# Perceiver layer on one core: the second product with the values moved behind the second burst of scores

## The chip, the cores and the metric

The kernel runs on one core of a Trainium2 chip. The metric is the time of one execution in microseconds (us) on the device, as a median over several runs. Lower is better. All arithmetic is in float32.

## The reference, cut to what matters

There are 32 sequences of 64 rows with 256 features. Each has a context of 1601 rows. Three blocks follow one another, each added to x: attention over the context with 16 heads of 16 features, an attention whose weights depend on positions, and a feed-forward block with a shared part and experts. The change touches the first one:

```python
qh = _split_heads(q @ wq_w.T + wq_b)          # q is the normalised x
kh = _split_heads(k @ wk_w.T + wk_b)          # k and v are the context
vh = _split_heads(v @ wv_w.T + wv_b)
scores = jnp.einsum('bhqd,bhkd->bhqk', qh, kh) / jnp.sqrt(jnp.float32(D_K))
scores = jnp.where(mask, scores, jnp.float32(-1000000000.0))
attn = jax.nn.softmax(scores, axis=-1)
out = jnp.einsum('bhqk,bhkd->bhqd', attn, vh)
```

## The kernel before

The context's 1601 rows (keys) are cut into 13 blocks of 124 and stand on the partitions once they have become scores. The work goes by halves: half n is a sequence b and a group c of eight heads, so there are 64 halves. The loop at line 766 runs over n = 0 to 62. One pass of it, called a stretch here, prepares scores for half n+1, turns the scores of half n into exponentials, and multiplies the exponentials of half n-1 with the values. The order on TensorE (PE), VectorE (DVE), ScalarE (ACT) and GpSimd (POOL) is the order in which the code records the instructions (`manual_schedule`, line 730); each engine works its queue strictly from the front.

TensorE's work in a stretch, in order, with the names that the profile shows:

- `values(n-1, 0)` (line 625), the first product of the exponentials with the values: 52 matmuls into the tile `pvs`, in column tiles (four matmuls side by side in four groups of 32 columns of the array).
- `project_keys(b+1, c, 0)`, tile `pk`: keys from the context. `product` (line 488) issues a projection either whole or in column tiles of 32 when `tiled` is true.
- `scores(n+1, 0)` (line 529): a burst of 16 matmuls in row tiles, tiles `psc`. Four key blocks for four pairs of heads, one bank of PSUM for each pair.
- `turned_maxima` (`pm`), a projection, `maxima_along_rows` (`pb`): the running maxima of half n are transposed, reduced by DVE (`mc`, line 601) and spread again.
- the steps of other layers that are due (`run`, line 695): generators that the agenda resumes at given stretches. They bring work such as `po`, `tr_q`, `tr_h`, `tr_f`.
- `values(n-1, 1)`, the second product, in column tiles.
- `scores(n+1, 1)`: the second burst, 20 matmuls. It has five key blocks; those of the fifth go to two banks of their own, called `more`. One is an ordinary bank. The other is `spare_pvs`, the second half of the tile `both` (lines 436 to 439) whose first half is `pvs`; the profile calls both halves `pvs`.
- projections of keys and values, whole, then the third burst `scores(n+1, 2)`, then projections in column tiles.

DVE takes the scores out of PSUM, adds the mask (line 570 for four blocks, line 563 for the fifth blocks) and updates the running maxima in `mrun` (line 587), in an order written out as strings. For the second burst it is one of these:

```python
    "A 0 m3 1 B 2 m8 3 m4 m5",
SOONER = "A 0 1 B 2 m8 3 m4 m5"
LATER = "A 0 m1 1 m2 B 2 m3 3 m8 m4 m5"
```

A digit is a bank with four blocks, m with a number is a maximum, A and B are the two banks with the fifth blocks. B is the one in `spare_pvs`. POOL subtracts the maxima (line 618), four pairs per half, and ACT takes the exponentials (line 623). ACT also copies projections out of PSUM with the bias (`kT`, line 507; `v`, line 524), copies `mb` (line 613) and starts the maxima (`mrun`, line 579). SyncE (SP) issues the loads of the context in four pieces per sequence, two sequences ahead (`piece_ahead`). Six banks of PSUM (`ps_x`) rotate among projections, scores and steps, so a matmul into a bank waits for whoever read it last.

Of the kernel before, what the change touches and what calls it, by code (L numbers as in the profile page):

```python
# [90 lines left out]
def perceiver_kernel(ctx: ExitStack, tc: tile.TileContext, a: dict[str, bass.AP], out: bass.AP):  # L91
# [16 lines left out]
    def mm_bank(name: str):  # L108
        return ps_mm.tile([P, 512], F32, tag="mm", name=name)
# [33 lines left out]
    def load_piece(b: int, g: int):  # L143
        c0, n = GROUPS[g]
        k0, kn = c0 * CHUNK, min(n * CHUNK, KEYS - c0 * CHUNK)
        ct = big.tile([P, 2, 4 * CHUNK], F32, tag="ct", bufs=5, name=f"ct_{b}_{g}")
        nc.sync.dma_start(
            out=ct[:, :, :kn],
            in_=a["ctxT"][b].rearrange("(c p) k -> p c k", p=P)[:, :, k0 : k0 + kn],
        )  # L150
        cts[b].append(ct)
# [269 lines left out]
    def pair_of(n: int, j: int):  # L421
        return prob[:CHUNK, place(n, j // 2), j % 2]
# [60 lines left out]
    def piece_ahead(b: int, g: int):  # L483
        if b < B:
            load_piece(b, g)
# [43 lines left out]
    def scores(n: int, g: int, then=None, order=None):  # L529

        b, c = halves[n]
        c0, nb = SCORED[g]


        more = [mm_bank(f"psc_{b}_{c}_{g}"), spare_pvs] if nb == 5 else None
        pss = [mm_bank(f"psc_{b}_{c}_{g}_{j}") for j in range(4)]
        for r in range(nb):
            for j in range(4):
                e, s = divmod(j, 2)[::-1]
                fifth = nb == 5 and r == 4 * s  # L540
                i = 4 if fifth else r - (nb == 5 and s == 0)
                ps, at = (more[e], s) if fifth else (pss[j], i)
                if fifth and j == 2:
                    tc.add_manual_dep(nc.tensor.nop().ins, mm.ins.name, IN_TURN, reason="banks")
                k0 = (c0 + i) * CHUNK
                product = nc.tensor.matmul(  # L546
                    ps[:CHUNK, at * P : (at + 1) * P],
                    lhsT=kTs[c][32 * j : 32 * j + 32, k0 : k0 + CHUNK],
                    rhs=qbd[b // 2][32 * j : 32 * j + 32, c, b % 2, :, :],
                    start=True, stop=True, tile_position=(32 * j, 0),  # L550
                )
                if fifth and j == 1:
                    mm = product
        held = then() if then else None
        for item in (order or ORDER[g]).split():
            if item == "t":
                if held is not None:
                    maxima_of_rows(*held)
            elif item[0] == "m":
                maximum(n, int(item[1:]))  # L560
            elif item in "AB":
                k, e = c0 + 4, "AB".index(item)
                nc.vector.tensor_tensor(  # L563
                    block_of(n, k)[:, :, e, :],
                    more[e][:CHUNK, : 2 * P].rearrange("p (r q) -> p r q", r=2),
                    madd_fifth[:CHUNK, None, :].to_broadcast([CHUNK, 2, P]), ALU.add,
                )
            else:
                j = int(item)
                nc.vector.tensor_tensor(  # L570
                    pair_of(n, j)[:, c0 : c0 + 4, :].rearrange("p k (e q) -> p k e q", e=2),
                    pss[j][:CHUNK].rearrange("p (k e q) -> p k e q", k=4, e=2),
                    madd[:CHUNK, c0 : c0 + 4, None, :].to_broadcast([CHUNK, 4, 2, S]), ALU.add,
                )
# [47 lines left out]
    def exponentials(n: int, j: int):  # L622
        nc.scalar.activation(pair_of(n, j), pair_of(n, j), AF.Exp)  # L623

    def values(n: int, r: int):

        b, c = halves[n]
        v = vs[b % 2]
        for k in range(NKC):
            kn = min(CHUNK, KEYS - k * CHUNK)  # L630
            for j in range(4):
                h = 4 * r + j
                nc.tensor.matmul(  # L633
                    pvs[32 * j : 32 * j + DK + 1, c, :, r, :],
                    lhsT=v[:kn, k, 8 * c + h, :],
                    rhs=pair_of(n, h // 2)[:kn, k, (h % 2) * S : (h % 2) * S + S],
                    start=(k == 0), stop=(k == NKC - 1), tile_position=(0, 32 * j),
                )
# [29 lines left out]
    def linear_factor(u: int):  # L668
        quarter, hc = divmod(u, NHC)
        nc.scalar.activation(  # L670
            gated_at(quarter, hc), half_unit(u, sw3), AF.Identity, bias=b3twice[:, hc : hc + 1]
        )
        linear.add(u)
# [29 lines left out]
    def finish_steps(b: int, stretch: int):  # L703

        t = b // 2
        if b % 2 == 0:
            oT[t] = work.tile([P, 2, 2, S], F32, tag="oT", name=f"oT_{t}")
        flat = "p c u r q -> p (c u r q)"
        nc.vector.transpose(turned_pvs.rearrange(flat), pvs.rearrange(flat))
        by_head = turned_pvs.rearrange("p c u r i -> p (c u r) i")  # L710
        rec = work.tile([P, 8], F32, tag="rec", name=f"rec_{b}")
        nc.vector.reciprocal(rec, by_head[:, :, DK])
        o = work.tile([P, 8, DK], F32, tag="o", name=f"o_{b}")
        nc.vector.tensor_tensor(
            o, by_head[:, :, :DK], rec[:, :, None].to_broadcast([P, 8, DK]), ALU.mult
        )
        nc.vector.transpose(oT[t][:, :, b % 2, :], o.rearrange("p (c n) i -> p c (n i)", c=2))
        if b % 2:
            at = steps_of(t)
            agenda[stretch - 1 + at[0]].append((t, span_steps(t, oT.pop(t))))  # L720
            held_at.add(stretch - 1 + at[SMALL])
        yield
# [39 lines left out]
        load_piece(1, g)  # L762
    last = len(halves) - 1

    extra = {3 * last - 3: (0,), 3 * last - 2: (1, 2, 4), 3 * last - 1: (5, 6)}
    for n, (b, c) in enumerate(halves[:-1]):
        if c == 0:
            piece_ahead(b + 2, 0)
            if b % 2 == 0 and b // 2 + 1 < NTILE:
                load_x(b // 2 + 1)  # L770
        if c and b % 2 == 0 and b // 2 + 1 < NTILE:
            agenda[3 * n].append((b // 2 + 1, query_steps(b // 2 + 1)))

        def project(f, *args):
            if b + 1 < B:
                f(b + 1, *args)

        def steps(g: int):
            run(3 * n + g)
            for u in extra.get(3 * n + g, ()):  # L780
                linear_factor(u)

        def taken_off():
            turned.extend(turned_maxima(n))
            return turned

        turned: list = []
        if n:
            values(n - 1, 0)
        project(project_keys, c, 0, True)  # L790
        if n:
            steps(-1)
            exponentials(n - 1, 3)
        if c:
            piece_ahead(b + 2, 1)
        scores(n + 1, 0, taken_off)
        if c:
            project(project_values, 3)
        else:
            project(project_keys, c, 1)  # L800
        m = maxima_along_rows(turned[1])
        less_maxima(n, 0, m, nc.gpsimd)
        held = 3 * n in held_at
        if not held:
            first_maxima(n + 1)
        run(3 * n)
        if n:
            values(n - 1, 1)
            if c == 0:
                agenda[3 * n + 1].append((b // 2, finish_steps(b - 1, 3 * n + 1)))  # L810
        for u in extra.get(3 * n, ()):
            linear_factor(u)
        if held:
            first_maxima(n + 1)
        else:
            for k in (1, 2) if c else (1, 2, 3):
                maximum(n + 1, k)

        scores(n + 1, 1, order=LATER if held else None if c else SOONER)
        exponentials(n, 0)  # L820
        if c:
            project(project_keys, c, 1)
            piece_ahead(b + 2, 2)
            project(project_values, 4)
            project(project_keys, c, 2)
            piece_ahead(b + 2, 3)
        else:
            project(project_keys, c, 2)
            for u in (0, 1):
                project(project_values, u)  # L830
        less_maxima(n, 1, m, nc.gpsimd)
        steps(1)
        exponentials(n, 1)

        less_maxima(n, 2, m, nc.gpsimd)
        scores(n + 1, 2)
        project(project_keys, c, 3, True)
        for u in (5, 6) if c else (2,):
            project(project_values, u, True)
        less_maxima(n, 3, m, nc.gpsimd)  # L840
        exponentials(n, 2)
# [177 lines left out]
```

## Time and profile before

| | |
|---|---|
| median of 3 runs | 1513.79 us (1511.66 to 1515.7) |
| the profiled execution | 1510.1 us, of which the span from first to last instruction is 1508.3 us |
| mean granted TensorE clock | 0.994 of full speed |
| instructions in the profile | 62981 |
| matmuls of L633 (both products with the values) | 212.3 us busy, 13312 records |
| matmuls of L546 into psc (scores) | 239.2 us busy, 6400 records |
| DVE L563 out of the half of `pvs` | 64 instructions, 415 ns each |

A float32 matmul leaves two records, so counts of records are twice those of matmuls. Busy time of TensorE counts overlapping matmuls once. "L546" is line 546 of the listing. The timeline merges equal instructions that follow each other: its columns are start, time from the first start to the last end, engine, line, operation, output and inputs, shape, and count; brackets tell idle time of the engine and what ended it.

### The profile page before, as it was taken

The numbers are of one execution on the slowest core, as the hardware profiler recorded it, in microseconds if no ns is written. First come the engines' busy times: TensorE is split into PE (matmuls) and PEld (weight loads), VectorE is DVE, ScalarE is ACT, GpSimd is POOL, SyncE is SP. The second block draws the span as 40 slices with busy tenths as digits, with TensorE's granted clock in tenths as the row PEclk, the third lists the DMA queues.
The fourth block names the chain that finished last, engine by engine and source line by source line (L and its number), as shares of the span: only waits on it lengthen the run. The fifth ranks groups of instructions, "written<-read, shape, count | busy, mean of one in ns | idle before, by whom it ended". The sixth has DMA issues, their size and how long they took to land.

```text
span 1508.3 us, 62981 instructions
## 1 busy us (share of the span) xinstructions
PE 1466.4 (97%) x28600; PEld 1059.0 (70%) x28600; DVE 1226.2 (81%) x2332; ACT 953.7 (63%) x1727; POOL 1120.2 (74%) x508
## 2 busy tenths in 40 slices
PE   8999999999999999999999999999999999988899
PEld 5676777777676767777777767777777777654587
DVE  4889898998989898989989899989899898973100
ACT  3565667676776767586767767676767666766411
POOL 1677787988878887879888888878798888852710
PEclk9999999999999999999999999999999999999999
DMA  5211111111111111111111111111111111005100
GB/s 179 56 37 46 36 47 46 38 48 50 50 50 47 43 43 43 37 53 37 49 51 50 50 47 52 34 44 37 52 46 40 50 50 33 2 9 161 60 29 28
DMA packets 52220, 73.95 MB, mean 49 GB/s; under 512 B 3828, under 2 KB 51184, under 8 KB 51824
## 3 DMA queue, kind: packets, MB, share of 16 engines
q1 hardware_dynamic: 51136, 69.13, 16.1%
q8 instruction: 225, 3.69, 1.0%
q10 hardware_dynamic: 816, 0.79, 0.2%
q14 instruction: 43, 0.35, 0.1%
HBM read 65.71 MB, written 4.19 MB: 46 GB/s over the span
## 4 chain that ended last, share of the span: by engine, by line
PE 58%; DVE 20%; POOL 11%; ACT 8%; issue 2%; DMA 0%; ACTq 0%; DVEq 0%; POOLq 0%
PE pv L492 14%; PE pk L492 13%; POOL prob L618 9%; DVE prob L570 8%; PE pvs L633 7%; PE psc L546 7%; DVE mrun L587 7%; PE py L949 4%; PE u L662 2%; PE pb L609 2%; PE ph L931 2%; DVE mc L601 2%; ACT prob L623 2%; ACT qbd L474 1%; PE psa L357 1%
## 5 line engine op out<-in xcount | busy, mean ns | idle before, releaser
L618 POOL TENSOR_TENSOR prob<-prob,mb 124x1664 f32<-124x1664 f32 x252 | 938.9, 3751 | 217.2 <-ACT mb L613 160.4
L570 DVE TENSOR_TENSOR prob<-psc,madd 124x512 f32<-124x512 f32 x768 | 505.4, 682 | 76.1 <-PE psc L546 75.8
L623 ACT ACTIVATE prob<-prob 124x1664 f32<-124x1664 f32 x256 | 407.1, 1590 | 214.9 <-POOL prob L618 212.0
L587 DVE TENSOR_TENSOR mrun<-prob,mrun 124x512 f32<-124x512 f32 x704 | 486.6, 691 | 31.1 <-ACT mrun L579 17.3
L492 PE MATMUL pk<-ct,wkT_sb 128*32 128x496 f32 (+1 forms) x2512 | 398.9, 519 | 7.5 <-DMA wkT_sb<-in_wkT 5.4
L492 PE MATMUL pv<-wvT_sb,ct 128*124 128x256 f32 x3524 | 386.1, 379 | 0.6 <-DVE prob L563 0.5
L492 PEld LDWEIGHTS pv<-wvT_sb,ct 128*124 128x124 f32 x3524 | 270.3, 132 | 108.1 <-issue 19.4
L546 PEld LDWEIGHTS psc<-qbd,kT 32*124 32x124 f32 x6400 | 201.0, 181 | 63.5 <-issue 19.2
L546 PE MATMUL psc<-qbd,kT 32*124 32x128 f32 x6400 | 239.2, 279 | 2.7 <-issue 1.4
L492 PEld LDWEIGHTS pk<-ct,wkT_sb 128*32 128x32 f32 (+1 forms) x2512 | 146.6, 126 | 118.3 <-issue 59.0
L633 PEld LDWEIGHTS pvs<-prob,v 124*17 124x17 f32 x13312 | 197.3, 98 | 29.9 <-issue 16.2
L633 PE MATMUL pvs<-prob,v 124*17 124x64 f32 x13312 | 212.3, 220 | 1.6 <-ACT prob L623 1.6
L507 ACT ACTIVATE kT<-pk,cols 128x372 f32<-128x372 f32 (+2 forms) x256 | 150.0, 586 | 81.9 <-PE pk L492 81.7
L524 ACT COPY v<-pv 124x512 f32<-124x512 f32 (+1 forms) x224 | 124.1, 554 | 85.4 <-PE pv L492 84.0
L323 ACT ACTIVATE sc<-sc,least 128x64 f32<-128x64 f32 x256 | 85.6, 342 | 2.1 <-DVE least L319 2.1
L951 DVE SCALAR_TENSOR_TENSOR ot<-py,prob 128x256 f32<-128x256 f32 x16 | 6.8, 425 | 75.7 <-PE py L949 66.1
L662 PE MATMUL u<-xfT,sw_sb 128*128 128x512 f32 x128 | 60.9, 624 | 3.6 <-ACT prob L689 2.7
L579 ACT COPY mrun<-prob 124x512 f32<-124x512 f32 x64 | 38.0, 593 | 38.3 <-DVE soft L306 35.3
L546 PE MATMUL pvs<-qbd,kT 32*124 32x128 f32 x256 | 55.2, 294 | 0.2 <-issue 0.2
L323 ACT ACTIVATION_READ_ACCUMULATOR sc<-sc,least 128x1 f32 x256 | 50.0, 195 | 0.0
L609 PEld LDWEIGHTS pb<-cst,mc 128*124 128x124 f32 x256 | 28.8, 135 | 29.3 <-DVE mc L601 23.8
L938 ACT ACTIVATE hT<-ph,cols 128x256 f32<-128x256 f32 x32 | 13.4, 471 | 56.3 <-PE ph L931 56.3
(126 smaller groups left out, 1249.3 us busy)
## 6 DMA issues: line engine op xcount, KB each, us to landing
ct<-in_ctxT SPq DMA_DIRECT2D x64, 372.0 KB, 3.2
ct<-in_ctxT SPq DMA_DIRECT2D x32, 496.0 KB, 3.7
ct<-in_ctxT SPq DMA_DIRECT2D x32, 361.0 KB, 3.2
w<-in_w SPq DMA_DIRECT2D x16, 256.0 KB, 7.2
x<-in_x SPq DMA_DIRECT2D x17, 128.0 KB, 2.7
x_kept<-x SPq DMA_DIRECT2D x16, 128.0 KB, 1.7
prob<-x_kept SPq DMA_DIRECT2D x8, 256.0 KB, 6.2
out<-ot SPq DMA_DIRECT2D x16, 128.0 KB, 1.9
```

Of the source, the lines that this page charges most:

```text
L323: nc.scalar.activation(sc[:, h, :], sc[:, h, :], AF.Exp, bias=least[:, h : h + 1], scale=-1.0, accum_out=total[:, h : h + 1],)
L492: nc.tensor.matmul(out[at:end], lhsT=lhsT[:, at:end], rhs=rhs, start=start, stop=stop, **(dict(tile_position=(0, at)) if tiled else {}),)
L507: nc.scalar.activation(kTs[c][:, k0 : k0 + kn], ps[:, :kn], AF.Identity, bias=cols[:, B_K + c : B_K + c + 1])
L524: nc.scalar.copy(vs[b % 2][:kn, 2 * u : 2 * u + n, :, :DK], ps[:kn, : n * D].rearrange("p (n h d) -> p n h d", n=n, d=DK),)
L546: product = nc.tensor.matmul(ps[:CHUNK, at * P : (at + 1) * P], lhsT=kTs[c][32 * j : 32 * j + 32, k0 : k0 + CHUNK], rhs=qbd[b // 2][32 * j ...
L570: nc.vector.tensor_tensor(pair_of(n, j)[:, c0 : c0 + 4, :].rearrange("p k (e q) -> p k e q", e=2), pss[j][:CHUNK].rearrange("p (k e q) -> ...
L587: nc.vector.tensor_tensor(dst, block_of(n, k), run, ALU.max)
L618: engine.tensor_tensor(sj, sj, m[:CHUNK, j, None, :].to_broadcast([CHUNK, NKC, P]), ALU.subtract)
L623: nc.scalar.activation(pair_of(n, j), pair_of(n, j), AF.Exp)
L633: nc.tensor.matmul(pvs[32 * j : 32 * j + DK + 1, c, :, r, :], lhsT=v[:kn, k, 8 * c + h, :], rhs=pair_of(n, h // 2)[:kn, k, (h % 2) * S : ( ...
L662: nc.tensor.matmul(ps, lhsT=w[:, c, hc * P : (hc + 1) * P], rhs=xfT[:, c, :, slot], start=(c == 0), stop=(c == 1),)
L949: nc.tensor.matmul(py, lhsT=x, rhs=w, start=(n == 0), stop=(n == len(terms) - 1))
```

## The change

The second product moves from ahead of the second burst of scores to behind it and behind the first projection there. All projections between the second burst and the third go in column tiles. The exponentials of the fourth pair of half n-1, which the second product needs, move on ACT from the stretch's beginning to behind the steps that are due. The projection of keys stands ahead of `exponentials(n, 0)` now, which changes ACT's order too. At the end of the loop seven linear factors of the feed-forward block (`linear_factor`) are given to other places.

```diff
-    extra = {3 * last - 3: (0,), 3 * last - 2: (1, 2, 4), 3 * last - 1: (5, 6)}
+    extra = {3 * last - 2: (0, 1, 2), 3 * last - 1: (4, 5, 6)}
...
         if n:
             steps(-1)
-            exponentials(n - 1, 3)
...
         run(3 * n)
         if n:
-            values(n - 1, 1)
-            if c == 0:
-                agenda[3 * n + 1].append((b // 2, finish_steps(b - 1, 3 * n + 1)))
-        for u in extra.get(3 * n, ()):
-            linear_factor(u)
+            exponentials(n - 1, 3)
+        if n and c == 0:
+            agenda[3 * n + 1].append((b // 2, finish_steps(b - 1, 3 * n + 1)))
...
         scores(n + 1, 1, order=LATER if held else None if c else SOONER)
+        if c:
+            project(project_keys, c, 1, True)
+            piece_ahead(b + 2, 2)
+        else:
+            project(project_keys, c, 2, True)
+        if n:
+            values(n - 1, 1)
         exponentials(n, 0)
         if c:
-            project(project_keys, c, 1)
-            piece_ahead(b + 2, 2)
-            project(project_values, 4)
-            project(project_keys, c, 2)
+            project(project_values, 4, True)
+            project(project_keys, c, 2, True)
             piece_ahead(b + 2, 3)
         else:
-            project(project_keys, c, 2)
             for u in (0, 1):
-                project(project_values, u)
+                project(project_values, u, True)
```

## The prediction

> **What bounds the kernel now.** First the page: the engines' shares and the chain that ended last.
>
> ```profile
> PE 1466.4 (97%) x28600; PEld 1059.0 (70%) x28600; DVE 1226.2 (81%) x2332; ACT 953.7 (63%) x1727; POOL 1120.2 (74%) x508
> ...
> PE 58%; DVE 20%; POOL 11%; ACT 8%; issue 2%; DMA 0%; ACTq 0%; DVEq 0%; POOLq 0%
> ```
>
> TensorE is busy nearly all the time, but DVE carries a fifth of the chain, so DVE is close behind. Then the timeline of TensorE over one stretch in the steady part (columns: start, us, engine, line, what, count). I call the start of its first burst of scores S; here S = 797.09.
>
> ```profile
> 797.09 1.15 PE L546 MATMUL psc<-qbd,kT 32*124 32x128 f32 x32
> ...
> 801.09 1.03 PE L251 MATMUL po<-woP_sb,oT 128*128 128x256 f32 x4
> 802.05 1.65 PE L633 MATMUL pvs<-prob,v 124*17 124x64 f32 x104
> 803.62 0.37 PE L546 MATMUL psc<-qbd,kT 32*124 32x128 f32 x1
> 803.63 0.37 PE L546 MATMUL pvs<-qbd,kT 32*124 32x128 f32 x1
> ...
> 804.93 1.52 PE L492 MATMUL pk<-ct,wkT_sb 128*128 128x372 f32 x4
> 806.28 1.89 PE L492 MATMUL pv<-wvT_sb,ct 128*124 128x256 f32 x8
> 808.01 1.41 PE L492 MATMUL pk<-ct,wkT_sb 128*128 128x372 f32 x4
> 809.35 1.15 PE L546 MATMUL psc<-qbd,kT 32*124 32x128 f32 x32
> 810.43 1.42 PE L492 MATMUL pk<-ct,wkT_sb 128*32 128x361 f32 x16
> 811.67 2.77 PE L492 MATMUL pv<-wvT_sb,ct 128*32 128x256 f32 x48
> 814.26 1.64 PE L633 MATMUL pvs<-prob,v 124*17 124x64 f32 x104
> 815.72 1.85 PE L492 MATMUL pk<-ct,wkT_sb 128*32 128x496 f32 x16
> 817.50 1.15 PE L546 MATMUL psc<-qbd,kT 32*124 32x128 f32 x32
> ```
>
> See that each group starts where the one ahead stops streaming: there is no slack to spend, so what TensorE has to wait is added to the time. See also who writes the tile `pvs`: the product with the values (L633), and at 803.63 the scores too, since one bank for the fifth blocks is the other half of that tile. Last, DVE over the same stretch:
>
> ```profile
> 803.24 1.19 DVE L319 TENSOR_REDUCE least<-sc 128x16 f32<-128x1024 f32 x1
> 804.34 1.42 DVE L587 TENSOR_TENSOR mrun<-prob,mrun 124x512 f32<-124x512 f32 x2
> 805.67 0.42 DVE L563 TENSOR_TENSOR prob<-psc,madd_fifth 124x256 f32<-124x256 f32 x1
> 806.00 0.68 DVE L570 TENSOR_TENSOR prob<-psc,madd 124x512 f32<-124x512 f32 x1
> 806.60 0.69 DVE L587 TENSOR_TENSOR mrun<-prob,mrun 124x512 f32<-124x512 f32 x1
> 807.20 0.68 DVE L570 TENSOR_TENSOR prob<-psc,madd 124x512 f32<-124x512 f32 x1
> 807.80 0.41 DVE L563 TENSOR_TENSOR prob<-pvs,madd_fifth 124x256 f32<-124x256 f32 x1
> ```
>
> DVE works through without a gap and clears the scores' half of `pvs` (I call this eviction B) only at 808.21, which is S+11.12, though those scores were written by 805.
>
> **The change, part by part.** *Tiles.* A projection of 256 columns in column tiles leaves 32 records instead of 8, four side by side, and streams for 1.73 us either way (8 whole records from 806.28 to 808.01; 48 tiled ones take 2.59 from 811.67 to 814.26, so 32 take 1.73): nothing. Changes between row tiles, column tiles and the whole array cost 0.09 to 0.13 each (a product with the values takes 1.58 ahead of scores and 1.46 ahead of tiled projections; a tiled projection of 496 columns takes 1.78 ahead of scores, 1.66 ahead of another tiled product). Pairing the product with tiled projections saves 0.17, 0.13, 0.09 and 0.06 us in the four kinds of stretch that repeat, 0.45 per four.
>
> *The moved product.* In the order of the changed program its first matmul waits for the eviction L563 that reads `pvs`, that is B of the same stretch. Before, the product stood ahead of that burst and had no such wait. Behind the product in TensorE's queue stand the remaining projections and the third burst, so all of these start late, and DVE and the next S with them. DVE's, GpSimd's and SyncE's orders are unchanged, and what DVE does between S and B hangs on S (the first evictions, the copy into mrun, po), so B keeps its distance from S. Scores that come earlier don't help, because DVE is busy until the first eviction: the idle time ahead of it is nothing in nearly every stretch.
>
> For one cycle of four stretches (S at 778.28, 797.09, 817.50, 839.95; 82.47 us), B ends at S+9.03, 11.12, 10.15 and 10.35. I add 0.06 from the eviction's end to TensorE's start (elsewhere the maxima in mc end at 820.61 and pb starts at 820.66), 1.46 for the product, the tiled projections left (two of values: 3.45; or one of values and one of keys: 1.73+1.28) and 0.10 to 0.12 for the change of tiles. The next group then starts at S+14.1, 15.8, 15.2 and 15.0; before it started at S+11.53 (scores), 12.26 (scores), 12.73 (pq) and 11.25 (psa). The loss is 2.6, 3.5, 2.5 and 3.7, or 12.3 per cycle; the saved changes of tiles are already in it. The same subtraction over all 61 stretches gives **+184 us**. Its bounds: nothing, if B comes before TensorE arrives; 12.3 x 15.25 = 188, if the early stretches are like the rest.
>
> *The clock.* TensorE now idles at one place in each stretch: it arrives at about S+6.8, 7.6, 8.2 and 7.0, so 2.3, 3.6, 2.0 and 3.4 us. The trace has the price of idling in its tail (columns: window, length, busy time of PE, ..., granted clock, DMA):
>
> ```profile
> 1337.46:1340.87 3.41, 0.98 (x36) 0.67 (x24) 2.62 (x4) 2.39 (x3) 2.00 (x2) 1.00 0.02 5
> 1340.87:1344.28 3.41, 2.64 (x65) 2.24 (x68) 1.42 (x2) 0.59 (x1) 0.00 (x0) 0.50 0.01 2
> 1354.53:1357.94 3.41, 1.98 (x105) 1.47 (x104) 1.26 (x5) 3.38 (x4) 0.00 (x0) 1.00 0.17 32
> 1357.94:1361.35 3.41, 3.25 (x10) 1.98 (x11) 2.28 (x6) 3.40 (x22) 0.77 (x2) 1.00 0.75 238
> ```
>
> The granted clock changes in steps of 3.41 us. After a window with 0.98 us of work it is 0.50; after one with 1.98 it stays 1.00; those at 1378.42 and 1392.07 had 0.76 and 1.34 and were followed by 0.50. So the limit lies between 1.4 and 2.1 us of idle time per window. A window at half clock costs at most 1.7 us. The long stalls (3.4 and 3.6) pass the limit in nearly every position, at some 1.3 us, since part of the slow window is still the stall; the short ones (2.0 and 2.3) in about half of the positions, at 1.6 (an estimate from where a stall of that length can lie across windows). That is 2 x 1.3 + 2 x 0.5 x 1.6 = 4.2 per cycle, 15.25 cycles, **+64 us**. The bounds are 0 and 61 x 1.7 = 104.
>
> The Trainium skill ("TensorE: Matmul & The Clock Gate", the table under "Why this matters for your kernels") tells to avoid idle gaps over about 3 us; by it only the two long stalls would pay, 15.25 x 2 x 1.3 = 40. The rows above show the drop after 2.1 to 2.4 us of idle time in a window, so I go by the rows. The skill's page "PSUM — Partial Sum Buffer" (the rule under "PSUM bank collisions raise a hardware error") says to guard by bank and quadrant and not by address. That speaks against this change: the two halves of `pvs` share no address; by addresses alone the moved product would owe B nothing and the 184 would be 0, by the rule it owes all of it, and no run of before shows such a wait.
>
> *ScalarE.* The exponentials of the fourth pair stand behind the copies of mb and mrun now. From mb's start at S+4 to S+4.5 I count 1.1 for both copies, 1.05 for the square or 2.1 for the small copies and exponentials where those stand there, and 1.6 for itself: the end lies between S+7.2 and S+8.8. B covers that; without B it would cost 0.6 to 0.8 us in two stretches of four. The first scores of the second burst lose their cover too: they wait for the last eviction of the first burst (S+4.31) or for copies, 0.5 to 0.8 us in three of four stretches, also inside the wait for B. *Rest.* SyncE's order is the same; the last piece of the context is issued some 3 us later, lands in 3.2 us, and is needed a pair of stretches on: nothing. The factors of the last stretches only trade places among TensorE's work: nothing, within 2 us.
>
> Sum: 1510.1 (profiled execution: span 1508.3 and 1.8 around it) + 184 + 64 = **1758**. The median of the runs shown is 1513.8, 0.2% above that execution, inside what a measurement tells (about 0.3%).
>
> **Rivals.** (1) The stall comes, the clock stays: 1510 + 184 = 1694. For it: all steady windows before are at 1.00, and windows with 1.4 us idle kept the clock. Against it: three windows of the tail. (2) B does not decide, but the lost covers do: 0.5 to 0.8 in three stretches of four (1.8), less 0.45 per four, with the late exponentials' 1.4 some 2.8 per cycle, times 15.25: 1553. It needs B to end 2 to 3.6 us sooner. (3) The other side: **faster**. If evictions ran early enough that B is done before TensorE arrives (S+6.7 to 7.6), only the saved changes of tiles remain, 0.45 x 15.25 = 7: 1503. For it: tile changes do cost 0.1 each in the rows. Against it: B ends at S+9.0 at the earliest in the repeating cycle, with DVE busy up to it. (4) Stalls and a clock that is slow for two windows each time: up to 1510 + 188 + 2 x 104 = 1906.
>
> **How the numbers follow.** Forecast 0.62, (1) 0.20, (2) 0.06, (3) 0.05, (4) 0.07. The forecast's own range, with the clock at 30 to 95 us, is 1724 to 1793; to hold 8 in 10 the range takes in rival (1) and part of (4): 1665 to 1850. Faster 0.05, same 0.02, slower 0.93.
>
> **What would show it.** TensorE's waits should name DVE L563 ahead of L633, once per stretch, 2 to 4 us each, some 170 to 180 us in total; TensorE's share falls below 90%; DVE's busy time stays near 1226 us. The granted clock should fall below 0.95, with many windows at 0.50. If it stays at 0.99, rival (1) holds. If L563 is no releaser of L633, I am wrong at the root.

## The result

| | before | changed |
|---|---|---|
| median | 1511.79 us (6 runs, 1507.76 to 1515.7) | 1768.86 us (6 runs, 1764.6 to 1777.89) |
| profiled execution, its span | 1510.1, 1508.3 us | 1765.97, 1764.2 us |
| mean granted TensorE clock | 0.994 | 0.946 |

The changed kernel takes 1.1704 times as long (95% interval 1.1669 to 1.1738). The forecast was 1758.

The page of the changed kernel, engines' shares and chain:

```profile
PE 1563.8 (89%) x31948; PEld 1047.6 (59%) x31948; DVE 1230.6 (70%) x2332; ACT 959.5 (54%) x1727; POOL 1119.8 (63%) x508
...
PE 69%; DVE 24%; ACT 4%; issue 2%; DMA 1%; POOL 0%; ACTq 0%; DVEq 0%; POOLq 0%
```

TensorE falls from 97% to 89% of a longer span. DVE's busy time hardly moves (1226.2 to 1230.6), so nobody else got more work. TensorE's busy time rises by 97 us although its arithmetic is the same. Its waits (columns: who, for whom, us in total, times, longest):

```profile
PE pvs L633 <- DVE prob L563: 166.0, 62, 4.5
PE pb L609 <- DVE mc L601: 7.3, 30, 1.5
```

The first row was not there before; the second was (7.2 us, 29 times). The first comes once for each of the 62 moved products; its total is a little under the 170 to 180 us that were expected. How one of them looks, on TensorE and on DVE (the stretch with S = 915.21, of the first kind of the cycle):

```profile
920.64 1.46 PE L492 MATMUL pk<-ct,wkT_sb 128*32 128x372 f32 x16
924.30 2.88 PE L633 MATMUL pvs<-prob,v 124*17 124x64 f32 x104 [2.21 <-DVE prob L563]
926.94 4.10 PE L492 MATMUL pv<-wvT_sb,ct 128*32 128x256 f32 x64
```

```profile
920.24 2.16 DVE L587 TENSOR_TENSOR mrun<-prob,mrun 124x512 f32<-124x512 f32 x3 [0.73 <-ACT mrun L579]
922.31 0.42 DVE L563 TENSOR_TENSOR prob<-psc,madd_fifth 124x256 f32<-124x256 f32 x1
922.64 1.28 DVE L570 TENSOR_TENSOR prob<-psc,madd 124x512 f32<-124x512 f32 x2
923.84 0.41 DVE L563 TENSOR_TENSOR prob<-pvs,madd_fifth 124x256 f32<-124x256 f32 x1
```

Eviction B ends at 924.25, S+9.04 (before: S+9.03), and the product starts 0.05 us later. Then read the product's own length: 104 records took 1.65 us before and take 2.88 here. The windows say why (columns as above: window, length, TensorE's busy time, ..., granted clock):

```profile
921.05:924.46 3.41, 1.20 (x28) 0.34 (x24) 3.38 (x7) 2.97 (x4) 3.41 (x2) 1.00 0.00 0
924.46:927.87 3.41, 3.41 (x116) 2.97 (x112) 3.34 (x6) 0.70 (x1) 3.41 (x2) 0.50 0.02 5
968.84:972.25 3.41, 2.40 (x47) 1.23 (x46) 3.31 (x8) 3.41 (x11) 3.41 (x2) 1.00 0.14 46
972.25:975.66 3.41, 2.38 (x124) 2.01 (x128) 3.38 (x7) 1.14 (x1) 3.24 (x3) 1.00 0.00 0
```

A window with 1.20 us of work is followed by a whole one at half clock, in which TensorE is busy all the time. Where a stall falls across two windows (968.84 and 972.25, 1.0 us idle in each) the clock stays.

### The profile page after: what moved, and what is told of

It reads as the page before. It is cut to its first block, busy times and chain, and to the rows that moved or that the text cites. A ratio compares the mean times of both kernels' runs of the same rounds, so it can differ in the third digit from the quotient of the medians.

```text
span 1764.2 us, 69691 instructions
## 1 busy us (share of the span) xinstructions
PE 1563.8 (89%) x31948; PEld 1047.6 (59%) x31948; DVE 1230.6 (70%) x2332; ACT 959.5 (54%) x1727; POOL 1119.8 (63%) x508
## 4 chain that ended last, share of the span: by engine, by line
PE 69%; DVE 24%; ACT 4%; issue 2%; DMA 1%; POOL 0%; ACTq 0%; DVEq 0%; POOLq 0%
PE pv L492 20%; PE pvs L633 13%; PE pk L492 13%; DVE prob L570 7%; PE psc L546 7%; DVE mrun L587 7%; PE py L950 3%; PE u L662 3%; DVE prob L563 2%; DVE mc L601 2%; PE ph L932 2%; PE pb L609 1%; PE pq L466 1%; PE pm L594 1%; PE psa L357 1%
## 5 line engine op out<-in xcount | busy, mean ns | idle before, releaser
L492 PE MATMUL pv<-wvT_sb,ct 128*32 128x256 f32 (+1 forms) x5756 | 422.8, 408 | 0.6 <-DVE prob L563 0.6
L623 ACT ACTIVATE prob<-prob 124x1664 f32<-124x1664 f32 x256 | 407.7, 1593 | 18.3 <-POOL prob L618 15.7
L492 PE MATMUL pk<-ct,wkT_sb 128*32 128x372 f32 (+4 forms) x3628 | 396.1, 506 | 5.7 <-DMA wkT_sb<-in_wkT 5.5
L633 PE MATMUL pvs<-prob,v 124*17 124x64 f32 x13312 | 253.7, 242 | 166.0 <-DVE prob L563 166.0
L633 PEld LDWEIGHTS pvs<-prob,v 124*17 124x17 f32 x13312 | 234.8, 110 | 221.1 <-DVE prob L563 207.4
L492 PEld LDWEIGHTS pv<-wvT_sb,ct 128*32 128x32 f32 (+1 forms) x5756 | 235.7, 123 | 151.3 <-issue 55.5
L546 PEld LDWEIGHTS psc<-qbd,kT 32*124 32x124 f32 x6400 | 213.5, 181 | 77.4 <-issue 34.3
L546 PE MATMUL psc<-qbd,kT 32*124 32x128 f32 x6400 | 255.5, 282 | 3.0 <-ACT qbd L474 0.9
L492 PEld LDWEIGHTS pk<-ct,wkT_sb 128*32 128x32 f32 (+1 forms) x3628 | 124.1, 113 | 131.6 <-issue 95.1
L609 PE MATMUL pb<-cst,mc 128*124 128x128 f32 x256 | 39.9, 279 | 7.4 <-DVE mc L601 7.3
```

The costliest lines, as they stand in the source:

```text
L492: nc.tensor.matmul(out[at:end], lhsT=lhsT[:, at:end], rhs=rhs, start=start, stop=stop, **(dict(tile_position=(0, at)) if tiled else {}),)
L546: product = nc.tensor.matmul(ps[:CHUNK, at * P : (at + 1) * P], lhsT=kTs[c][32 * j : 32 * j + 32, k0 : k0 + CHUNK], rhs=qbd[b // 2][32 * j ...
L609: nc.tensor.transpose(ps[:CHUNK, j * P : (j + 1) * P], col[:, j : j + 1].to_broadcast([P, CHUNK]), ident)
L633: nc.tensor.matmul(pvs[32 * j : 32 * j + DK + 1, c, :, r, :], lhsT=v[:kn, k, 8 * c + h, :], rhs=pair_of(n, h // 2)[:kn, k, (h % 2) * S : ( ...
```

## The experiments

Theory: the moved product waits for the eviction of the bank half beside it, and the idle time takes the clock down as well. Rivals: the column tiles cost; the late exponentials hold the product; the clock has no part.

**Tiles alone.** The kernel before, with only the projections changed:

```diff
-            project(project_keys, c, 1)
+            project(project_keys, c, 1, True)
...
-            project(project_values, 4)
-            project(project_keys, c, 2)
+            project(project_values, 4, True)
+            project(project_keys, c, 2, True)
...
-            project(project_keys, c, 2)
+            project(project_keys, c, 2, True)
...
-                project(project_values, u)
+                project(project_values, u, True)
```

> The kernel before, with all projections between the second and the third burst in column tiles, the product with the values left ahead of the second burst. Theory (the wait for the eviction of the shared bank does it): tiles stream as fast as whole projections and the changes of tiles are worth 0.01 to 0.05 us in a stretch, so 1505 to 1515 us, clock 0.99. Rival (the tiles themselves cost, through 1674 more matmuls and weight loads): well above, towards the 1769 of the changed kernel.

Measured: 1509.53 us, 0.9983 of the kernel before (0.9969 to 0.9997), clock 0.995. The 1674 more matmuls cost nothing; the tiles are rather worth 0.17%.

**The move alone.** The changed kernel with those same `True` taken out again.

> The changed kernel, with the projections between the second and the third burst whole again. Theory: the wait for the eviction of the shared bank is the same, about 165 us; a product with the values now stands between whole projections and pays 0.1 to 0.2 us more in a stretch for changes of tiles: 1765 to 1790 us, clock 0.94 to 0.95. Rival (tiles cost): near the kernel before, 1510 to 1600.

Measured: 1787.89 us, ratio 1.1814 (1.1759 to 1.1868), clock 0.931. The wait is there as it was:

```profile
PE pvs L633 <- DVE prob L563: 162.5, 62, 4.5
```

So the loss is there without the tiles, and the tiles take a little of it back. Where the clock is full, a whole projection starts 1.58 us after the start of the product ahead of it, a tiled one 1.47; over 62 products that is 7 of the 19 us between the two kernels. The rest goes with the clock, which was under the expected 0.94 to 0.95 in most of the runs (0.931 to 0.940): in its trace 72 windows run at half clock, in the changed kernel's 56. Why stalls that are no longer took the clock down more often there, no run tells.

**The eviction moved forward.** In the changed kernel, B first among the second burst's evictions:

```diff
-SOONER = "A 0 1 B 2 m8 3 m4 m5"
-LATER = "A 0 m1 1 m2 B 2 m3 3 m8 m4 m5"
+SOONER = "B A 0 1 2 m8 3 m4 m5"
+LATER = "B A 0 m1 1 m2 2 m3 3 m8 m4 m5"
...
-    "A 0 m3 1 B 2 m8 3 m4 m5",
+    "B A 0 m3 1 2 m8 3 m4 m5",
```

> The changed kernel, with the eviction of the shared bank first among the second burst's evictions on DVE, where the eviction of the other extra bank stood. By the rows of before it ends 1.5, 2.1, 1.5 and 2.7 us sooner in the four kinds of stretch, 7.8 per four, 119 us in all; what is left of the stalls is under 1.5 us and keeps the clock. Theory: 1510 + 184 - 119 = 1575, up to 1600, clock over 0.98. Rival (another wait, such as the late exponentials, holds the product): 1680 or more. Rival (1) with no part for the clock: 1769 - 119 = 1650, clock still under 0.96.

Measured: 1571.43 us, ratio 1.0382 (1.0348 to 1.0416), clock 0.995. One letter moved in each of DVE's three orders gives back 197 us. In the waits of this kernel the row is still there, shorter:

```profile
PE pvs L633 <- DVE prob L563: 43.7, 57, 1.8
```

No wait is over 1.8 us, and the clock is whole. No engine has more or less to do than in the changed kernel. That excludes the tiles and the late exponentials as the main cause: both are as in the changed kernel.

**The wait filled with needless work.** In the changed kernel the projection ahead of the product is computed two or three times into the same bank, so that the result is the same:

```diff
-        for i in range(2):
+        for i in range(2 * times):
             product(
-                ps[:, :kn], wkT[:, i, c * P : (c + 1) * P], cts[b][g][:, i, :kn],
-                i == 0, i == 1, tiled,
+                ps[:, :kn], wkT[:, i % 2, c * P : (c + 1) * P], cts[b][g][:, i % 2, :kn],
+                i % 2 == 0, i % 2 == 1, tiled,
...
-            project(project_keys, c, 1, True)
+            project(project_keys, c, 1, True, 3)
...
-            project(project_keys, c, 2, True)
+            project(project_keys, c, 2, True, 2)
```

> The changed kernel, with the projection ahead of the moved product computed more than once into the same bank: twice in the stretches with c = 0, three times in those with c = 1, so TensorE does 1.24 or 2.48 us of work that changes nothing while it would wait. Theory (idle time drops the clock, and the clock's share is about 64 us): the wait left is about 1 us, the clock stays over 0.985, and the time falls to about 1694 us although more work is done (1680 to 1715). Rival (the clock's share is nothing, or it isn't idle time that lowers it): 1769 or more.

Measured: 1691.6 us, ratio 1.1182 (1.1151 to 1.1212). The kernel does more and takes 77 us less. Its page and its waits:

```profile
PE 1603.8 (95%) x33436; PEld 1044.5 (62%) x33436; DVE 1231.0 (73%) x2332; ACT 959.0 (57%) x1727; POOL 1122.9 (66%) x508
```

```profile
PE pvs L633 <- DVE prob L563: 52.2, 56, 4.5
```

```profile
core 0: 1690.1 us, clock 0.994
```

Counted from S, the product starts no earlier (S+9.10 in the first kind of stretch, as in the changed kernel); what is gained is the clock alone. So the two terms are apart: 1691.6 - 1511.6 = 180 us for the wait and what comes with it, 77 for the clock. The length of a cycle of four stretches, from S to S, tells the same: on the mean of the eight cycles from n = 16 to 47 it is 82.8 us before, 94.8 here and 99.7 in the changed kernel, so 12.0 for the wait and 4.9 for the clock.

**The eviction at once.** As the kernel with B first, and B also ahead of the running maxima that DVE did in front of it:

```diff
-            for k in (1, 2) if c else (1, 2, 3):
-                maximum(n + 1, k)
+            early = " ".join(f"m{k}" for k in ((1, 2) if c else (1, 2, 3)))
 
-        scores(n + 1, 1, order=LATER if held else None if c else SOONER)
+        scores(n + 1, 1, order=LATER if held else f"B {early} " + (ORDER[1] if c else SOONER)[2:])
```

> The kernel with the eviction of the shared bank first, with that eviction also ahead of the running maxima that stood in front of it (in the stretches where those stand elsewhere, nothing more changes). DVE then frees the shared bank as soon as the scores are written and its earlier work is done. Theory: of the 44 us of idle time that L563 still causes, some 10 to 15 us stay (DVE's other work in two of four stretches); the late exponentials come out from behind it with 0.6 to 0.8 us in two stretches of four (about 20 us), and the second burst's own waits (19 us) stay: 1530 to 1560. Rival (the rest has nothing to do with the eviction): 1571.

Measured: 1554.78 us, ratio 1.0293 (1.0278 to 1.0308), clock 0.995. What holds the product now:

```profile
PE pvs L633 <- ACT prob L623: 12.8, 29, 1.5
PE pvs L633 <- DVE prob L563: 9.7, 16, 1.8
```

The late exponentials (L623) come out from behind the eviction, as expected, in half of the stretches. From its start to the next group the second burst takes 1.64 us on the mean, 1.37 in the kernel before: 16 us over the 62 stretches, for banks that are not free yet. That is more than the 7 us which the saved changes of tiles were estimated at, so a product that waits for nothing of its own would probably still not pay at this place; no run has such a product there.

**The product further back.** In the changed kernel, for c = 1 alone, the product behind the other two projections:

```diff
-        if n:
+        if n and not c:
             values(n - 1, 1)
         exponentials(n, 0)
         if c:
             project(project_values, 4, True)
             project(project_keys, c, 2, True)
             piece_ahead(b + 2, 3)
+            values(n - 1, 1)
```

> The changed kernel, with the moved product behind the other two projections in the stretches with c = 1; those with c = 0 stay as they are. Theory: there the projections lie beside the wait (1.73 + 1.28 us), which leaves 0.4 to 0.6 us of it; the two other kinds of stretch still lose 2.6 and 2.5 us. Sum 6.3 us per four stretches, 95 us, and the clock's part of the two short stalls, some 30 us: 1634, between 1605 and 1655, clock between 0.96 and 0.985. Rival (the place in the queue doesn't matter, only the later eviction): 1769.

Measured: 1631.26 us, ratio 1.0797 (1.0775 to 1.0819), clock 0.986. Waits of L633 for L563:

```profile
PE pvs L633 <- DVE prob L563: 66.4, 31, 4.5
```

Of 62 waits 31 are left, those with c = 0. With c = 1 the projections lie beside the wait. They meet a wait of their own there, though: the projection of values waits for the eviction of the bank that it is to have, which held the other fifth blocks (A).

```profile
PE pv L492 <- DVE prob L563: 26.1, 29, 1.6
```

So the sum agrees with its forecast partly by luck. With c = 1 some 18 us were left in it, and this wait is 26; the clock was put at 30 us, and the trace has 13 windows at half clock against 5 before, worth about 15 (half of TensorE's busy time in them). (With c = 0 this can't be done: the values that the product reads are overwritten by the projections behind it.)

**A version meant to beat both.** For c = 0 as in tiles alone. For c = 1:

```diff
-            exponentials(n - 1, 3)
+            if not c:
+                exponentials(n - 1, 3)
...
-        if n:
+        if c:
+            project(project_keys, c, 1)
+            piece_ahead(b + 2, 2)
+            exponentials(n - 1, 3)
+        elif n:
             values(n - 1, 1)
...
         if c:
-            project(project_keys, c, 1, True)
-            piece_ahead(b + 2, 2)
             project(project_values, 4, True)
             project(project_keys, c, 2, True)
             piece_ahead(b + 2, 3)
+            values(n - 1, 1)
```

with B second among the evictions of those stretches ("A B 0 ...").

> A kernel meant to beat both: with c = 0 as in the kernel with tiles alone; with c = 1 a whole projection of keys stands ahead of the second burst (it covers the banks that are not free yet, and needs no change of tiles behind the transposes), then the burst, the other two projections in tiles, and the product last ahead of the third burst; the shared bank is evicted second. Theory: the eviction ends before the product's turn in both kinds of stretch, 0.2 and 0.1 us of tile changes are saved, 15.25 times: 1504, between 1500 and 1509. Rival (the late exponentials or the eviction still hold the product): above 1515.

Measured: 1508.62 us, ratio 0.9982 (0.9971 to 0.9992). L633 no longer waits for L563 at all, and the time is 0.18% under that of before: no better than tiles alone, and 2 of the 7 us that the forecast of 1504 stood for. In the two traces it is 3.3 us ahead of tiles alone at the start of the last first burst (1312.0 against 1315.3 us from the span's start), and it gives 3 us back behind that; why, no run here tells.

## Why the prediction was right

- *The moved product waits for B, and B keeps its distance from S.* Right. In the four kinds of stretch B ends at S+9.04, 10.85, 10.16 and 10.33, against 9.03, 11.12, 10.15 and 10.35 before; only the second kind moved, by 0.27. The stalls are 2.21, 3.46, 2.05 and 3.21 us, against 2.3, 3.6, 2.0 and 3.4. The eviction is the releaser in all 62 cases. Whether the chip needs this wait or only the program's order sets it, no run tells, since none leaves it out.
- *184 us for it.* Measured 180, as the difference of the kernel with the filled wait and the one before. In the changed kernel's trace it is 166.0 us of idle time ahead of the product and 19 us by which the second burst itself got longer (85 to 104 us over 62 stretches), since the product no longer covers the banks it waits for, less a few for the saved changes of tiles.
- *64 us for the clock.* The mechanism was right, the term too small: 77. Of the 28 stalls over 3 us 27 took the clock down, of the 30 between 2.0 and 2.5 us 18 did; so "nearly every position" and "about half" were near. Within the loop 174 us run at half clock, 51 windows, or 3.3 in a cycle of four stretches; I had 3. And in these TensorE is busy for 160 of the 174 us, where I took a quarter of a slow window after a long stall to be still the stall. Half of 160 is 80 by the trace; in the kernel before no window of the loop is at half clock. The two errors have one sign, the 4 us of the first term the other, so that the total of 1758 is nearer than the clock's term.
- *Tiles cost nothing.* Right: 1509.5. With the product at its old place they are worth 2 us.
- *The late exponentials are covered by B.* Right as long as B is late. With B at once they cost 12.8 us, of the 21 that I had (0.6 and 0.8 us in 15 cycles).
- Rival (1), the clock untouched, would have been 1694; the kernel with the filled wait shows this number, 1691.6, as what the wait alone costs. Rival (2), the lost covers, needs B sooner and put its price at 1553; with B at once it is 1554.78, but in other parts (9.7 us of it are still the wait for B, and the covers and exponentials are less than it had). Rival (3), faster, needs B before TensorE's arrival. With B at once only 16 of the 62 waits for B are left, and the lost covers and the late exponentials still hold the time above that of before. Rival (4), two slow windows for each stall: only 8 of the 56 windows at half clock follow another one.

## What to carry to other kernels

When a step is moved, look for what it now follows in memory, bank by bank, and not only in data: here two halves of one tile that share no address shared a bank, and the wait was the distance between two orders written by hand, on two engines. Work out when the releasing engine gets to the release, from a point that both engines share. Then count a stall on TensorE by its length and also by what it does to the clock: here every 100 us of waiting cost 43 more, and work without any use, put into the wait, was faster than waiting.

## What was not expected of the hardware

The limit of idle time is narrower than the trace of before could tell. Over the nine traces, windows of 3.41 us at full clock were followed by another at full clock with up to 2.01 us idle (the product further back), and by one at half clock from 1.79 us on (the eviction at once). Between these it went either way, so the busy time of the profile, in which the matmuls' ends are modelled, doesn't settle it alone. To get the clock back takes more work in a window than to keep it: a window at half clock with under 0.5 us idle was always followed by one at full clock, one with over 1.1 us never, and between 0.59 and 1.05 us it went either way.
